# Expert blocks of 64 rows, four rounds of routing and a list-scheduled tail in a graph-layer kernel

## The chip, the cores and the metric

The kernel runs on one core of a Trainium2 chip. The metric is the device time of one execution in microseconds; the figure for a kernel is the median of several runs. A profile is one further execution with the hardware profiler on. The names of the engines are those of the profile: PE (TensorE, with PEld for its weight loads), DVE (VectorE), ACT (ScalarE), POOL (GpSimd) and SP (SyncE, which only issues DMAs here).

## The reference

One layer on 6,250 nodes of 256 features and 106,250 directed edges that are sorted by their target. It adds a message-passing part and a linear attention to the nodes, and then a feed-forward part in which each node goes to one of 32 experts.

```python
xn = _layernorm(x, axis=-1)
x = x + gnn(xn, edge_index, edge_attr_64, W, b, gamma, beta) + mix(xn[None], Wqkv, Wout, bout)[0]
x = x + ffn(_layernorm(x, axis=-1)[None], router_w, router_b, W1, b1, W2, b2)[0]

# gnn
msgs = jnp.concatenate([node_features[source], edge_features], axis=-1)
msgs = jax.nn.silu(msgs @ W + b)
out = jax.ops.segment_sum(msgs, target, num_segments=N)      # then a layer norm with gamma, beta
# mix: 8 heads of 64; k and v are normalised per head
dots = jnp.einsum('bhnd,bhne->bhde', k, v)
out = jnp.einsum('bhnd,bhde->bhne', q, dots) / n             # then Wout and bout
# ffn: one expert per token
idx = jnp.argmax(xf @ router_w.T + router_b, axis=-1)
h = relu(einsum('nd,ndh->nh', xf, W1[idx]) + b1[idx])        # 256 -> 64
out = relu(einsum('nh,nhd->nd', h, W2[idx]) + b2[idx])       # 64 -> 256
```

## The kernel before

**Tiles and stages.** The nodes lie in 49 tiles of 128 rows; `X` holds the running result and `wide` a second copy of each tile (first the transposed layer norm, later the normalised input of the experts), both in SBUF for the whole time. A first stage makes the layer norm, its transposed form in `wide` and the projection `proj` (stored in DRAM). It also tests whether the edges are laid out as the fast path needs. The result of that test is read into registers, and a branch chooses between `ordered` (the fast path) and `general` (a slow path for any edges).

**The edge loop.** `ordered` walks over 208 groups of 512 edges. Per group SP loads the edge features `ea` (line 1198), POOL gathers four times 128 rows of `proj` (`gat`, line 1213), PE turns `ea` (1229) and multiplies it (`h`, 1356), DVE adds (1360), ACT applies silu (1377). Every second group PE sums messages in two levels (`po`, line 1308, with four column tiles, then `sum`, line 1335). When the last edge of a node tile is through, `close` takes its sum (lines 182 and 617). Since the edges are sorted, tile t closes at about the fraction (t + 1)/49 of the loop.

**Other work between the groups.** After each group `work.step` lets a planner (class `Work`) advance other work, which is written as generators. Each step of a generator yields its estimated cost on PE and on DVE and a delay in groups; a group has a budget of 2.7 us on PE and 3.8 us on DVE (`ALLOWANCE`), which is moved a little between odd and even groups. Budget that is left over is dropped. Indirect DMAs of this work wait in a list `work.pool` and are put on POOL's queue beside the gathers, two after every second gather. The pieces are the attention (25 batches of two node tiles, lines 456 to 504, then `mix`, lines 505 to 541), the chunks of four to six closed tiles (add the attention, line 649 and 650; layer norm; router; rank of each token in its expert, lines 636 to 735), and the rounds.

**Rounds of experts.** The tiles are routed in three rounds, of 24, 16 and 9 tiles. For rounds 0 and 1, `places` gives each expert as many blocks of 128 rows as it needs, the tokens are sent to these rows with an indirect DMA per tile (`send`, line 854), and `experts` computes two blocks at a time: it loads the rows (`xb`, 873) and, per block, an expert's weights by a register value (`wt`, 938) from a table `wtab` that was copied together in DRAM beforehand. `layers` transposes (894, 896), multiplies (`phid` 902, `hid` 911) and multiplies again (`py` 923); the bias is a further matmul (945), and line 953 takes the result, which is stored in `yso` (967). Round 2 is an "own" round: each expert has one block of its own, and its weights stay in SBUF (`own_weights`, loaded on ACT's queue after the edge loop). Its bias is added later, at line 1041.

**The tail.** `collect` fetches the result of each tile with an indirect DMA (1024), adds it to `X` (1049, or 1041 to 1045 in the own round) and stores the tile (1052). All collecting comes after the edge loop. There `work.drain` runs the planner without budgets: in each turn every piece that is due is advanced, in the order of the list, and delays count turns. At the end a count of rows that did not fit is read into registers (`lacking`, 1555), and a second branch (1557) would redo the rounds in `again`.

Of the kernel before, what the change touches and what calls it, by code (L numbers as in the profile page):

```python
# [17 lines left out]
P = 128  # L18
# [13 lines left out]
CHUNKS = (6, 6, 6, 6, 6, 5, 5, 5, 4)  # L32
CH = max(CHUNKS)
FIRST = (3, 6, 10, 10, 10, 10)
AB = 2
BB = 2
LEAD = 3
AHEAD = 4
BESIDE = 2
ALLOWANCE = (2.7, 3.8)  # L40


ROUNDS = ((24, 44), (16, 38), (9, None))
# [11 lines left out]
def kernel(  # L55
# [167 lines left out]
    counting = const.tile([P, 3, P], BF16, name="counting")  # L223
    nc.vector.tensor_copy(counting[:, 2, :], ident)
# [18 lines left out]
    row_of = const.tile([P, NQ], F32, name="row_of")  # L243
    flag = const.tile([1, 1], I32, name="flag")
# [31 lines left out]
    with tc.tile_pool(name="prep", bufs=2) as prep, tc.tile_pool(name="pre_ps", bufs=2, space=PSUM) as pre_ps:  # L276
# [88 lines left out]
        nc.vector.tensor_copy(flag, pb)  # L365
# [43 lines left out]
    WROW = DC * HID + D  # L409
    wtab = dram.tile([NE, P, WROW], F32, name="wtab")  # L410

    def tabulate(engine, e0, e1):
        q = slice(e0, e1)
        a = DC * HID
        engine.dma_start(
            wtab[q, :, :a].rearrange("e p w -> (e p) w"), w1[q, :, :].rearrange("e (p c) h -> (e p) (c h)", c=DC)
        )
        for i in range(BB):
            engine.dma_start(wtab[q, i * HID : (i + 1) * HID, a:], w2[q, :, :])

# [3 lines left out]
    def weights(pool, bank, w):  # L424
# [3 lines left out]
        w.update(kv_w=kv_w, dots=dots)  # L428
        nf = 2 * F // P
        raw = pool.tile([P, nf, D], F32, tag="kv", name="raw", bufs=2)  # L430
        nc.sync.dma_start(raw, wqkv[F:, :].rearrange("(f p) c -> p f c", p=P))
        rawr = pool.tile([NE, D], F32, tag="sq", name="rawr")
# [3 lines left out]
        for f in range(0, nf, 2):  # L436
            pt = bank("t", [P, DC, 2, P], "pt")
            for c in range(DC):
                for i in range(2):
                    nc.tensor.transpose(pt[:, c, i, :], raw[:, f + i, c * P : (c + 1) * P], ident)  # L440
            nc.scalar.copy(kv_w[:, :, f * P : (f + 2) * P], pt.rearrange("p c i e -> p c (i e)"))
            yield 0.5, 0.0, 0
# [15 lines left out]
    def attention_batch(pool, bank, w, t0, t1):  # L458
# [3 lines left out]
        kv = pool.tile([P, AB, 2, F], F32, name="kv", bufs=2)  # L462
        var = small.tile([P, AB * 2 * HEADS], F32, name="var")
        for j in range(m):
            for s in range(2):
# [5 lines left out]
                nc.scalar.copy(kv[:, j, s, :], b)  # L471
                yield 1.9, 0.0, 1
            sq = pool.tile([P, 2 * HEADS, DH], F32, name="sq")
            nc.scalar.activation(sq, kv[:, j].rearrange("p s (h d) -> p (s h) d", d=DH), AF.Square)  # L474
# [11 lines left out]
        for j in range(m):  # L486
            k = kv[:, j, 0, :].rearrange("p (h d) -> p h d", d=DH)
            nc.vector.tensor_mul(k, k, both[:, j, :, None].to_broadcast([P, HEADS, DH]))
        yield 0.0, 1.4, 1
        pd = bank("t", [P, HP, DH], "pdot")  # L490
        for h in range(HP):
            for j in range(m):
                for i in range(2):
# [3 lines left out]
                        kv[:, j, 0, q],  # L497
                        kv[:, j, 1, q],
# [4 lines left out]
        nc.vector.tensor_add(dots, pd, dots)  # L503
        yield 0.6 * m, 0.4, 0

    def attention_matrix(pool, bank, w):

        raw = pool.tile([P, 2, HP, D], F32, tag="kv", name="raw", bufs=2)
        wq, rawo = raw[:, 0], raw[:, 1].rearrange("p h c -> p (h c)")
# [4 lines left out]
        made = pool.tile([P, 2, HP, D], F32, tag="kv", name="made", bufs=2)  # L514
        qd, wo_t = made[:, 0], made[:, 1]
        diag = pool.tile([P, HP, P], F32, tag="sq", name="diag")
# [26 lines left out]
    class Nodes:  # L543


        def __init__(self, pool, bank, rounds, in_order):
# [10 lines left out]
            self.so_far = pool.tile([P, BB, NE], F32, name="so_far")  # L557
# [4 lines left out]
            most = (N + (P - 1) * NE) // P + BB  # L562
            self.number = pool.tile([BB * NE, most], F32, name="number")
# [7 lines left out]

            self.upto = pool.tile([BB * NE, BB * NE], F32, name="upto")
            self.b2_sb = pool.tile([BB * NE, D], F32, name="b2_sb")
            nc.vector.memset(self.upto, 0.0)
            for i in range(BB):
                q = slice(i * NE, (i + 1) * NE)
                nc.vector.tensor_add(self.upto[q, q], after[q, q], ident[q, q])
                nc.sync.dma_start(self.b2_sb[q, :], b2)
# [24 lines left out]
            self.at = {}  # L603

        def clear(self, r, b0, b1):
            nc.sync.dma_start(
                r.xs[b0 * P : b1 * P, :].rearrange("(b p) d -> p b d", p=P),
                zero[:, None, :].to_broadcast([P, b1 - b0, D]),
# [24 lines left out]

        def chunk(self, t0, t1):
# [11 lines left out]
            for t in range(t0, t1):  # L646
                p = self.bank("kv", [P, D], "pres")
                for c in range(DC):
                    nc.tensor.matmul(p, xnT(t, c), mix[:, c, :], start=(c == 0), stop=(c == DC - 1))
                nc.vector.tensor_add(X[:, t, :], p, X[:, t, :])  # L650
                moments(mv2, t - t0, X[:, t, :])
                yield 0.9, 1.0, 0
            self.at[t0] = 1
            yield 0.0, 0.0, 1
# [3 lines left out]
            yield 0.0, 2.2, 1  # L658
# [64 lines left out]
            nc.tensor.matmul(pr[:, 1, 0, :], ones[0:1, :], self.so_far[0:1, 0, :], start=True, stop=True)  # L723
# [9 lines left out]
            nc.vector.tensor_copy(self.so_far, ahead[:, None, :, m].to_broadcast([P, BB, NE]))  # L733
            nc.vector.tensor_mul(logit, logit, hot)
            nc.vector.tensor_reduce(self.rank[:, t0:t1], logit, axis=AX.X, op=ALU.add)
            yield 1.2, 2.2, 1
            self.at[t0] = 3
            if r.own:
                row = small.tile([P, CH], F32, name="place")
                nc.vector.scalar_tensor_tensor(  # L740
                    row[:, :m], top[:, :m], float(-P), self.rank[:, t0:t1], op0=ALU.mult, op1=ALU.add
                )
                nc.vector.tensor_scalar_add(row[:, :m], row[:, :m], float(NE * P))
# [863 lines left out]
```

## Time and profile before

| | us |
|---|---|
| Median of three runs | 1425.22 |
| Lowest and highest | 1421.08, 1427.03 |
| The profiled execution | 1422.18 |
| Its span, first to last instruction | 1420.5 |
| PE busy | 1118.7 (79%) |
| POOL busy | 939.6 (66%) |
| DVE busy | 851.6 (60%) |
| ACT busy | 541.2 (38%) |
| First gather of the edge loop starts | 103.97 |
| Last gather starts | 1217.50 |
| Last matmul of the attention matrix starts (line 537) | 669.5 |
| Tokens are sent | 40 tiles before the last gather, 5 from 1235, 4 from 1302 |
| Results are fetched (line 1024) | from 1246.23 |
| Last store is issued (line 1052) | 1402.55 |

A row of a group of instructions has the line, engine and operation, what is written from what, how often, the busy time in us and the mean of one in ns, then the time for which the engine was idle just before them and what ended that idleness ("issue": nothing that the profile shows). A row of the order of time has the start, the duration, the instruction and in brackets the idle time before it. A row of the table of stages has a stretch of time, its length, the busy time and the number of instructions of PE, PEld, DVE, ACT and POOL (or of the one engine asked for), the TensorE clock granted (1.00 is full), the busy share of the DMA engines, and GB/s.

### The profile page before, as it was taken

The page shows a single profiled execution, that of the slowest core. Times are in us where ns is not written, and L with a number is a line of the kernel's source. Part 1 is how long each engine was busy: PE and PEld are TensorE (multiplying, and loading weights), DVE is VectorE, ACT ScalarE, POOL GpSimd, SP SyncE. Part 2 cuts the span into 40 slices and gives each one's busy share as a digit, 9 for nine tenths or more (in the row PEclk, how much of TensorE's full clock was granted, in tenths as well). Part 3 has the DMA queues.
Part 4 walks back from the last instruction along what each step waited for, and adds up shares of the span by engine and source line. Part 5 has one row for each costly group of instructions (what it writes and reads, how often), then busy time and mean ns, then how long its engine had stood idle before and what let it go on. Part 6 is the DMA issues. An engine that isn't in the chain of part 4 may idle for free.

```text
span 1420.5 us, 22703 instructions
## 1 busy us (share of the span) xinstructions
PE 1118.7 (79%) x7340; PEld 656.5 (46%) x7340; DVE 851.6 (60%) x2256; ACT 541.2 (38%) x987; POOL 939.6 (66%) x1050
## 2 busy tenths in 40 slices
PE   4876898899988888988987875489889766857862
PEld 3653444445444444545654543255555433534440
DVE  6933766767766676677876773256556644435342
ACT  2543555455445444543333332134344322212120
POOL 3537777777777777777777777777777677316222
PEclk9997999999999999999999877599999797866585
DMA  7238777655555554445444444478887546589672
GB/s 242 78 107 234 203 198 213 198 172 168 160 156 169 159 170 131 130 131 164 133 127 134 132 119 121 143 203 243 250 241 217 139 118 191 160 244 282 210 242 71
DMA packets 251813, 245.16 MB, mean 173 GB/s; under 512 B 130176, under 2 KB 221736, under 8 KB 251676
## 3 DMA queue, kind: packets, MB, share of 16 engines
q0 software_dynamic: 44960, 121.67, 29.3%
q1 hardware_dynamic: 196152, 113.91, 27.3%
q10 hardware_dynamic: 10564, 7.95, 1.9%
q8 instruction: 63, 1.03, 0.3%
q14 instruction: 74, 0.61, 0.2%
HBM read 194.34 MB, written 55.38 MB: 176 GB/s over the span
## 4 chain that ended last, share of the span: by engine, by line


## 5 line engine op out<-in xcount | busy, mean ns | idle before, releaser
L1213 POOL DMA_INDIRECT gat<-proj,src_T x831 | 796.8, 959 | 266.4 <-issue 219.8
L1360 DVE TENSOR_TENSOR gat<-h,gat 128x1024 f32<-128x1024 f32 x208 | 254.1, 1222 | 280.2 <-PE h L1356 148.0
L1377 ACT ACTIVATE gat<-gat 128x1024 f32<-128x1024 f32 x208 | 219.8, 1057 | 242.9 <-DVE gat L1360 205.8
L1356 PE MATMUL h<-ge,eT 64*128 64x256 f32 x1664 | 251.6, 423 | 33.2 <-DVE gat L1360 32.3
L1356 PEld LDWEIGHTS h<-ge,eT 64*128 64x128 f32 x1664 | 155.0, 198 | 137.1 <-issue 98.8
L1335 PE MATMUL sum<-part,s 128*128 128x256 f32 x400 | 129.6, 452 | 93.3 <-DVE s L1324 93.0
L468 PE MATMUL kv<-kv_w,wide 128*128 128x512 f32 x392 | 188.0, 606 | 3.2 <-DVE kv_w L450 3.2
L1233 ACT COPY eT<-pt 128x256 f32<-128x256 f32 x208 | 77.3, 371 | 204.6 <-PE pt L1229 195.0
L1335 PEld LDWEIGHTS sum<-part,s 128*128 128x128 f32 x400 | 78.7, 215 | 144.8 <-DVE s L1324 129.0
L1308 PE MATMUL po<-gat,s 128*32 128x256 f32 x1664 | 130.8, 439 | 0.0
L1024 POOL DMA_INDIRECT ot<-yso,back x49 | 48.5, 990 | 101.3 <-DVE wide L688 28.0
L1317 ACT COPY part<-po 128x256 f32<-128x256 f32 x104 | 38.7, 372 | 187.2 <-PE po L1308 187.2
L1229 PE MATMUL pt<-ident,ea 128*128 128x128 f32 x416 | 93.7, 308 | 2.2 <-DMA ea<-in_edge_attr_dram 1.4
L468 PEld LDWEIGHTS kv<-kv_w,wide 128*128 128x128 f32 x392 | 68.4, 193 | 57.5 <-issue 52.3
L475 DVE TENSOR_REDUCE var<-sq 128x16 f32<-128x1024 f32 x49 | 59.7, 1218 | 52.1 <-ACT sq L474 52.0
L896 DVE COPY xbT<-pt 128x512 f32<-128x512 f32 x57 | 39.2, 688 | 73.9 <-PE pt L894 73.7
L1308 PEld LDWEIGHTS po<-gat,s 128*32 128x32 f32 x1664 | 47.8, 121 | 67.7 <-issue 35.8
L1229 PEld LDWEIGHTS pt<-ident,ea 128*128 128x128 f32 x416 | 42.8, 144 | 75.2 <-issue 50.0
L854 POOL DMA_INDIRECT xso<-wide,slot x49 | 49.3, 1006 | 27.1 <-DVE back L770 16.7
L299 POOL TENSOR_TENSOR X<-X,bo 128x256 f32<-128x256 f32 x49 | 35.5, 746 | 47.7 <-ACT xn L296 25.9
L894 PE MATMUL pt<-ident,xb 128*128 128x128 f32 x228 | 49.2, 349 | 21.6 <-DMA xb<-xso 19.9
L306 PE MATMUL pp<-gw,wide 128*128 128x256 f32 (+1 forms) x196 | 53.5, 417 | 13.8 <-ACT wide L303 6.6
(264 smaller groups left out, 1391.7 us busy)
## 6 DMA issues: line engine op xcount, KB each, us to landing
ea<-in_edge_attr_dram SPq DMA_DIRECT2D x207, 128.0 KB
xb<-xso SPq DMA_DIRECT2D x57, 256.0 KB
xso<-zero SPq DMA_DIRECT2D x28, 512.0 KB
wt<-wtab SPq DMA_DIRECT2D x72, 192.0 KB
gat<-proj,src_T POOLq DMA_INDIRECT x831
yso<-xb SPq DMA_DIRECT2D x41, 256.0 KB
wtab<-in_L_ffn_W_dram SPq DMA_DIRECT2D x24, 256.0 KB
out_dram<-ot SPq DMA_DIRECT2D x48, 128.0 KB
```

What stands on the lines that cost most here:

```text
L306: nc.tensor.matmul(pp[:n, :], xnT(t, c, n), gw[:, c, :], start=(c == 0), stop=(c == DC - 1))
L468: nc.tensor.matmul(b, xnT(t0 + j, c), kv_w[:, c, s * F : (s + 1) * F], start=(c == 0), stop=(c == DC - 1))
L475: nc.vector.tensor_reduce(var[:, j * 2 * HEADS : (j + 1) * 2 * HEADS], sq, axis=AX.X, op=ALU.add)
L854: ins = nc.gpsimd.indirect_dma_start(out=r.xs[:], out_offset=bass.IndirectOffsetOnAxis(ap=self.slot[:n, t : t + 1], axis=0), in_=wide[:n, ...
L1213: nc.gpsimd.indirect_dma_start(out=gat[:n, k % 2, k // 2, :], out_offset=None, in_=proj[:], in_offset=bass.IndirectOffsetOnAxis(ap=src_T[: ...
L1229: nc.tensor.transpose(pt[:, j, :], ea[:, 2 * j : 2 * j + 2, :].rearrange("p k d -> p (k d)"), ident)
L1233: nc.scalar.copy(eT, pt)
L1308: nc.tensor.matmul(po[k * wide_k : (k + 1) * wide_k, :], s1[:, k, :], msg[:, k % 2, k // 2, :], start=(g == here[0]), stop=(g == here[-1]) ...
L1335: nc.tensor.matmul(sums[t], s2[:, (t - lo) * P : (t - lo + 1) * P], part, start=(q == opens[t]), stop=(q == closes[t]),)
L1356: nc.tensor.matmul(h[:, s, j, :], eTs[g][half, j, :], ge[half, :], start=True, stop=True)
L1360: nc.vector.tensor_add(gats[g], h, gats[g])
L1377: nc.scalar.activation(gats[g], gats[g], AF.Silu)
```

## The change

- Expert blocks have 64 rows (`HB`) in place of 128. `layers` works on a quad of four blocks: two tiles of 128 rows, in each of which the upper and lower half belong to different experts. Its matmuls are written to 64 columns of the array each, and the bias matmuls now stand ahead of `py`, in all rounds.
- There are four rounds, of 28, 11, 5 and 5 tiles, with room for 76 and 44 blocks in the first two. The last two are own rounds, with 64 rows for each expert. The chunks are (6, 6, 5, 5, 6, 6, 5, 5, 3, 2).
- The table `wtab` is gone. `experts` loads `w1` and `w2` of each block with two DMAs from the inputs. The own weights are loaded on SP's queue, during the edge loop, into tiles of `wide` whose tokens have been sent.
- `collect` fetches into 12 tiles of `wide`, adds into `X` and stores two tiles with one DMA.
- PE budget of up to 1.5 us is carried to the next group (`CARRY`); some delays of a group are gone; tokens are put on POOL's list as soon as their chunk has its places; the attention's part of later tiles (`mixing`) is added early.
- `drain` keeps a planned time for PE, DVE and POOL. It advances the first piece, urgent ones first, that is due and whose engine is planned to be free within 1 us.
- The branch ahead of the edge loop is gone: the result of the first test and the count of rows that did not fit are added into one flag, which is read after the tail. If it is set, `general` computes all again from the inputs. The arm `again` for the rounds is gone.
- The attention keeps `kv` in four buffers of one tile each in place of two of two tiles, has two buffers for the squares `sq`, and begins a batch a group after the last where it was three.

```diff
-CHUNKS = (6, 6, 6, 6, 6, 5, 5, 5, 4)
+CHUNKS = (6, 6, 5, 5, 6, 6, 5, 5, 3, 2)
+KV = 4
+HB = 64
+QB = 2 * BB
+AHEAD_US = 1.0
+CARRY = (1.5, 0.0)
-ROUNDS = ((24, 44), (16, 38), (9, None))
+ROUNDS = ((28, 76), (11, 44), (5, None), (5, None))
+BACK = (32, 44)
...
-            sq = pool.tile([P, 2 * HEADS, DH], F32, name="sq")
-            nc.scalar.activation(sq, kv[:, j].rearrange("p s (h d) -> p (s h) d", d=DH), AF.Square)
+            sq = pool.tile([P, 2 * HEADS, DH], F32, name="sq", bufs=2)
+            nc.scalar.activation(sq, kv[j].rearrange("p s (h d) -> p (s h) d", d=DH), AF.Square)
...
+        def mixings(self, t0, t1):
+
+            for t in range(t0, t1):
+                if t not in self.mixed:
+                    self.mixed.add(t)
+                    self.mixing(t)
+                    yield 0.9, 0.4, 1
...
+            ph = self.bank("kv", [P, QB // BB, HB], "phid")
+            for j in pairs:
+                for c in range(DC):
+                    for i in range(BB):
+                        nc.tensor.matmul(
+                            ph[i * HID : (i + 1) * HID, j, :],
+                            w1_of(BB * j + i, c),
+                            xbT[:, j, c, i * HB : (i + 1) * HB],
+                            start=(c == 0),
+                            stop=(c == DC - 1),
+                            tile_position=(0, i * HID),
+                        )
...
+                    nc.tensor.matmul(
+                        py[j][i * HB : (i + 1) * HB, :],
+                        one_of(BB * j + i).to_broadcast([NE, HB]),
+                        self.b2_sb,
+                        start=True,
+                        stop=False,
+                        tile_position=(0, i * HB),
+                    )
...
+                    nc.tensor.matmul(
+                        py[j][i * HB : (i + 1) * HB, :],
+                        hid[half, j, :],
+                        w2_of(BB * j + i, half),
+                        start=False,
+                        stop=True,
+                        tile_position=(i * HID, i * HB),
+                    )
...
-                last = queue.dma_start(w[:, i, :], wtab[bass.ds(e, 1), :, :].rearrange("o p w -> p (o w)"))
+                queue.dma_start(
+                    wa[:, b : b + 1, :], w1[bass.ds(e, 1), :, :].rearrange("o (p c) h -> p o (c h)", c=DC)
+                )
+                last = queue.dma_start(
+                    wb[i * HID : (i + 1) * HID, j : j + 1, :], w2[bass.ds(e, 1), :, :].rearrange("o h d -> h o d")
+                )
...
+        def own_weights(self):
+
+            for q in range(NE // QB):
+                e = slice(QB * q, QB * (q + 1))
+                while not all(self.work.turn >= self.gone.get(t, 1 << 30) + 3 for t in range(QB * q, QB * (q + 1))):
+                    yield 0.0, 0.0, 1
+                nc.sync.dma_start(
+                    wide[:, QB * q : QB * q + 2, :].rearrange("p t (b w) -> p (t b) w", b=2),
+                    w1[e, :, :].rearrange("e (p c) h -> p e (c h)", c=DC),
+                )
+                nc.sync.dma_start(
+                    wide[:, QB * q + 2 : QB * (q + 1), :], w2[e, :, :].rearrange("(j i) h d -> (i h) j d", i=BB)
+                )
+                self.weights_in += 1
+                yield 0.0, 0.0, 2
...
             for t, n, ot in got:
...
+                nc.vector.tensor_add(X[:n, t, :], ot[:n, :], X[:n, t, :])
             yield 0.0, 0.5 * len(got), 1
-            for t, n, ot in got:
-                nc.sync.dma_start(out[t * P : t * P + n, :], ot[:n, :])
+            move_rows(nc.sync, X[:, t0:t1, :], t0, t1, out, True)
...
         def drain(self):
+
             self.draining = True
             while self.pool:
-                self.pool.pop(0)()
+                self.issue(self.pool.pop(0))
+            for piece in self.pieces + self.urgent:
+                piece.due = self.now
             while self.pieces or self.urgent:
-                self.step((1e9, 1e9))
+                for piece in self.urgent + self.pieces:
+                    busy = (self.pool_free if piece.on_pool else max(self.free)) - self.now
+                    if piece.due <= self.now and (piece.urgent or busy <= AHEAD_US):
+                        self.advance(piece)
+                        break
+                else:
+                    self.now += 0.2
...
-    unlike = nc.values_load(flag[0:1, 0:1], min_val=0, max_val=1 << 20)
-    with tc.If(unlike < 1) as path:
...
+    with ExitStack() as arm:
+        with tc.manual_schedule():
+            ordered(arm)
+    wrong = nc.values_load(flag[0:1, 0:1], min_val=0, max_val=1 << 20)
+    with tc.If(wrong > 0):
         general()
```

## The prediction

> **What bounds the kernel now.** The chain of waits is empty for this execution, so I read the costliest groups, then the table of stages, then the order of time at both ends.
>
> ```profile
> L1213 POOL DMA_INDIRECT gat<-proj,src_T x831 | 796.8, 959 | 266.4 <-issue 219.8
> ```
>
> The gathers of the edge loop run on POOL; the gap before most of them waits for nothing. POOL's part of the order of time shows the step and the end of the loop:
>
> ```profile
> 1215.00 0.95 POOL L1213 DMA_INDIRECT gat<-proj,src_T  x1 [0.30 <-PE po L1308]
> 1216.25 0.95 POOL L1213 DMA_INDIRECT gat<-proj,src_T  x1 [0.30 <-issue]
> 1217.50 0.89 POOL L1213 DMA_INDIRECT gat<-proj,src_T  x1 [0.30 <-issue]
> ...
> 1235.17 1.05 POOL L854 DMA_INDIRECT xso<-wide,slot  x1 [16.70 <-DVE back L770]
> ```
>
> A gather takes a step of 1.25 us. From 103.97 to 1218.4 POOL does 831 gathers (1039 us) and 40 sends at 1.31 (52 us): 1091 of 1114 us. So POOL paces the loop, 5.0 us a group of four; only 23 us is lost. The stages (us, busy PE, PEld, DVE, ACT, POOL, then clock, DMA share, GB/s):
>
> ```profile
> 920.00:1120.00 200.00, 174.17 (x1289) 105.92 (x1282) 113.60 (x265) 81.84 (x169) 148.01 (x157) 0.95 0.77 225
> ...
> 1246.00:1302.00 56.00, 36.33 (x204) 22.85 (x203) 26.93 (x92) 9.26 (x27) 17.85 (x18) 0.68 0.89 270
> 1302.00:1332.00 30.00, 22.46 (x101) 12.31 (x100) 6.31 (x13) 6.34 (x18) 11.01 (x15) 0.50 0.74 228
> 1332.00:1383.00 51.00, 39.44 (x257) 24.48 (x256) 22.98 (x48) 11.83 (x32) 15.38 (x16) 0.77 0.75 238
> 1383.00:1403.00 20.00, 8.37 (x14) 3.46 (x14) 7.69 (x19) 0.00 (x0) 9.14 (x9) 0.57 0.41 124
> 1403.00:1420.00 17.00, 0.00 (x0) 0.00 (x0) 0.00 (x0) 0.00 (x0) 0.00 (x0) 0.50 0.09 18
> ```
>
> While round 0's experts run (920 to 1120) POOL keeps its step and PE has 26 us left. After 1218 no engine is full, and 202 us pass: round 1's pairs until 1331, the own pairs to 1383, their nine fetches to 1403, then 17 us with no work. This tail is what the change can shorten.
>
> **The skill.** "TensorEngine Tiling (Array Packing)", Tiling Modes (Key Properties), says that tiles of the array run loads and matmuls in parallel and that a change of mode drains TensorE. The trace agrees with the first: from 300 to 400 us, 176 passes of po (four column tiles) keep PE busy 11.78 us, 67 ns each, where 44 passes of sum on the whole array take 12.02 us, 273 ns. No row shows the drain. "TensorE: Matmul & The Clock Gate", Part 1, says that idling PE falls to half its clock: 0.50 stands at 1302 to 1332, and the slowest phid pass is 477 ns against 273. "Runtime: NRT & Kernel Launch", Instruction fetch mechanics, says that a taken branch out of the fetched pages must fetch its target. At the end (line 1557) it shows:
>
> ```profile
> L1557 PEldq COMPARE_BRANCH  x2: 3382/4670/5957, 1403.3 to 1406.9; - x2
> ```
>
> **The change, part by part.** Where the planner places work I count its groups, at 5.0 us each plus 1.31 for each send.
>
> *The first branch goes.* Worth 0. POOL passed it at 96.2 and then waited 11.1 us until 102.41 for DVE's row_of before its first iota, which stays ahead of the first gather. Bounds: 0 to 2 us gained, since the load of ea must land too.
>
> *Attention.* Two sq buffers take away at most the 52.0 us that DVE waited for sq at line 475, and the batches follow each other sooner. DVE and ACT are not the pace there, PE nearly is (494.79 of 566 us). Last mix matmul: 670. Round 0 now closes its tile 27 at about group 119, 104 + 119 x 5 + 15 = 714. Cost 0, hidden by POOL's step; if PE fills up, each us is lost in the loop. Bounds: -5 to +25.
>
> *Tables and clears.* 24 copies of 256 KB go, and the cleared rows fall from 14,592 to 11,776. DMA share is 0.60 there, so 0.
>
> *Expert blocks.* 57 pairs become 46 quads (19 + 11 + 8 + 8). A pair of round 0 costs PE, from the 920 to 1120 rows of its lines: transposes 15.57/21, phid 15.09/22, py 18.57/22, bias 15.92/22, together 3.0 us. A quad has the same transposes (0.74); phid has twice the passes at half the columns (16 x 36 ns, the pace of pdot's 160 passes in 5.76 us: 0.6); bias and py have twice the passes in two tiles each, 0.72 and 0.84 if they overlap, twice that if not. So 2.9 to 4.5 us; I take 3.1, since po shows overlap. SP pays more: a fetched block is two DMAs of 0.355 and a register load, about 0.4 (two fetches took 1.5), so 4 x 1.1 + 0.85 for tokens and result = 5.3 us a quad, against 2.4 a pair. At 8.3 us a pair (22 pairs from 918 to 1100) SP still has room: 5.3 + 0.7 for ea.
>
> *Rounds moved into the loop.* Sends inside it go from 40 to 47 (28 + 11 + 5 + 3): +9 us. Round 1's last tile (38) closes at group 166: 104 + 830 + 37 (28 sends) + 15 = 986; about 60 us to rank and send; 11 quads at 8.3 end near 1140. Round 2's tile 43 closes at group 187, near 1105; ranked by 1140, its 8 quads (weights already in wide) end near 1210. PE over 885 to 1229: 66 groups x 2.9 (h, pt, po, sum) + 38 x 3.1 + 25 for the chunks = 334 of 344 us. It just fits, so I add 2 us of stall. New end of the gathers: 1218 + 9 + 2 = 1229.
>
> *Own weights, mixings, returns.* The own weights move from ACT's queue after the loop (8 DMAs) to SP's inside it (16 DMAs, 16 x 0.36 = 6 us of issue, 4.2 MB over some 200 us), into tiles of wide. Each waits for the sends of its four tiles, and the next loads of ea stand behind it; the planner keeps three groups, 15 us, between, while a send takes 1.31 and lands within a few us: 0, up to 15 if a send is late. The pres matmuls of tiles 28 to 48 (51.4/49 = 1.05 us each, 22 us) run once mix is there, in PE's share of 670 to 860 (158.03 of 190), out of the last chunk's chain; carried PE budget fills such groups too. Returns get 12 buffers for 6, free once DVE has added them, so POOL no longer waits for a store to land (5.6 us in all); 49 stores become 25 or 26, which saves SP 23 x 0.37 = 9 us that other engines cover. All this is in the sums below.
>
> *The tail.* Its chain is now only round 3: (a) last gather to last sum: before 28 us (L617 ends at 1246.7), with experts between; the last group's h came 7 us after the gather, and the closing steps now follow at once, 7 more: 14. (b) Last sum to sends: 56 us before. Its DVE steps are some 35 of 0.16 to 0.6 us, 12 us, plus transposes and hops, 5, plus collect work between, 3: 20. (c) Two sends, landing and token load: 2.6 + 5.4 = 8; round 0 needed 3.2 from token issue to transposes. (d) Eight quads: a pair took 51/16 = 3.2 us at clock 0.77; per quad 3.1 to 5, I take 4: 33 with fill. (e) Last result to last store: 20.1 before for nine fetches (1382.4 to 1402.55), less four at 1.25: 15. (f) What follows: 18 before, one PE branch of 3.4 to 6.0 less: 13. Sum 103, so the span is 1229 + 103 = 1332. The 44 other fetches need 44 x 1.25 = 55 us of POOL, 1229 to 1284, and must let (b)'s sends in: +6 for one that does not. 1338; the profiled run was 1422.18 for a span of 1420.5: 1340. The median stands 3 us above it: **1343**.
>
> What is late next: POOL's fetches end near 1315 with the sends between, so they come 10 us before (e). The own weights no longer load at 1247 to 1263, when the DMA share is 0.89.
>
> **Rivals.** *As above*, 1343, chance 0.50. *A fuller tail*: PE, 97% booked by my sum, does not finish 11 + 8 quads in the loop. If all 19 spill, 19 x 4 = 76 us follow the gathers, where 42 us (a to c) is free: +34, and 6 more for the cold clock: 1383. For: before, round 1's sends came only at 1145, 130 us after its last tile could close. Against: its 16 tiles shared groups with 22 pairs, now 11 share with 19. Chance 0.25. *A shorter tail*: ranking 15, quads at 3.1, branches 6 less, no POOL collision: 1343 - 5 - 7 - 6 - 6 and 10 for better packing: 1309. Chance 0.11. *Slower*: SP's queue. Loads of ea stand in order behind 8 weight DMAs, 4 register loads and waits on ACT (SP waited 143 us for xb at line 967). If a quad holds up the edge loop, 38 of them pay; below 83/38 = 2.2 us each the tail's gain wins, above it the kernel is slower. SP waiting out ACT for 3 us a quad gives 38 x 3 = 114: 1457. For: 5.3 us of issue beside a group of 5.0. Against: ea is loaded four groups ahead, 20 us. Chance 0.14. *Not doing what it says*: a block overflow would run the general path. The router's counts with these inputs are 70 blocks of 76 and 38 of 44, and at most 51 and 45 tokens of 64 for an expert, so no.
>
> **The numbers.** What this measurement can tell from no change is about 0.5%, 7 us. The likeliest has its own range of 1315 to 1372. For 8 in 10 I go to 1303 to 1405: below lies half of the short-tail case, above the slow one. Faster 0.83 (the first three, less 0.03 near the bound), same 0.03, slower 0.14.
>
> **What would show it.** Last gather at 1220 to 1240, 44 to 47 sends before it; L896 done for rounds 0 to 2 by then; last sum 14 us after the last gather; 8 quads in about 33 us; under 14 us after the last store. Wrong if POOL's gathers step over 1.3 us on average while experts run, or if SP's waits stand before ea in PE's idle time.

## The result, and the profile after

The changed kernel takes 1443.38 us (median of four runs, 1439.15 to 1445.90), the kernel before 1426.12 in runs beside it: a ratio of 1.0118, 95% interval 1.0074 to 1.0162. It is slower by 1.2%; the forecast was 1343. The profiled execution took 1439.15 us for a span of 1437.2.

The tail did become shorter, from 202 us after the last gather to 132. But the edge loop ends 87 us later. First POOL's part of the order of time of the changed kernel (start, duration, instruction, in brackets the idle time before it):

```profile
1304.64 0.89 POOL L1223 DMA_INDIRECT gat<-proj,src_T  x1 [0.31 <-issue]
...
1344.77 1.01 POOL L874 DMA_INDIRECT xso<-wide,slot  x1 [6.65 <-DVE back L790]
...
1360.50 1.00 POOL L874 DMA_INDIRECT xso<-wide,slot  x1 [0.23 <-DVE X L1057]
...
1361.80 1.77 POOL L874 DMA_INDIRECT xso<-wide,slot  x1 [0.21 <-issue]
```

The last gather starts at 1304.64 (1217.50 before); the last two tiles are sent 56 us later. The costliest group, with the idle time that POOL has before its gathers:

```profile
L1223 POOL DMA_INDIRECT gat<-proj,src_T x831 | 797.7, 960 | 345.3 <-issue 305.5 <-PE pt L1239 13.4 <-PE h L1363 4.3
```

A gather takes as long as before (960 ns, 959 before). The idle time before gathers rose from 266.4 to 345.3 us, by 79: POOL is no longer the pace of the loop. The table of stages (us, then busy time and instructions of PE, PEld, DVE, ACT and POOL, then clock, DMA share, GB/s) says where:

```profile
200.00:300.00 100.00, 86.29 (x594) 45.63 (x590) 66.98 (x163) 46.90 (x73) 71.45 (x75) 0.91 0.50 139
...
960.00:1160.00 200.00, 151.18 (x1226) 90.59 (x1226) 88.06 (x214) 65.23 (x144) 115.16 (x123) 0.86 0.71 203
...
1373.00:1412.00 39.00, 34.61 (x288) 20.20 (x288) 9.88 (x21) 9.55 (x32) 7.60 (x8) 0.74 0.58 190
1412.00:1428.00 16.00, 0.00 (x0) 0.00 (x0) 1.92 (x5) 0.31 (x1) 5.35 (x5) 0.57 0.31 93
1428.00:1437.00 9.00, 0.00 (x0) 0.00 (x0) 0.20 (x1) 0.00 (x0) 0.00 (x0) 0.50 0.06 17
```

From 960 to 1160, while the fetched experts run, POOL issues 119 gathers and 2 sends (each send has a short `MEMSET` ahead of it, which makes the 123). At steps of 1.25 and 1.31 us that is 151 of 200 us; most of the rest is 12 gaps, 52 us in all. PE is busy for 151 of 200, so no engine is full. In the attention (200 to 300) POOL issues 75 gathers where it issued 80 in the kernel before:

```profile
200.00:300.00 100.00, 87.28 (x620) 46.01 (x612) 66.14 (x154) 47.83 (x76) 75.93 (x80) 0.94 0.69 195
```

By 850 us the changed kernel is 17 gathers behind the kernel before, by 1200 us, sends counted, 49. The last three rows of the changed kernel's table are the end of the tail: round 3's eight quads, then their fetches, then 9 us with next to no work (17 us with none before).

How a group loses its time is seen at 1041 to 1051 us. SP's queue of the changed kernel, from one load of tokens (`xb`) to the next:

```profile
1041.22 0.53 SPq L1208 DMA_DIRECT2D ea<-in_edge_attr_dram  x1
1041.84 0.46 SPq L962 DMA_DIRECT2D yso<-xb  x1
1042.35 0.46 SPq L888 DMA_DIRECT2D xb<-xso  x1
1044.04 0.36 SPq L979 DMA_DIRECT2D w1t<-in_L_ffn_W_dram  x1
1044.64 0.48 SPq L982 DMA_DIRECT2D w2t<-in_L_ffn_W_dram  x1
1045.89 0.36 SPq L979 DMA_DIRECT2D w1t<-in_L_ffn_W_dram  x1
...
1050.58 0.53 SPq L1208 DMA_DIRECT2D ea<-in_edge_attr_dram  x1
1051.16 0.50 SPq L888 DMA_DIRECT2D xb<-xso  x1
```

And PE and POOL of the same stretch:

```profile
1042.89 0.69 PE L918 MATMUL phid<-xbT,w1t 128*64 128x64 f32 x6 [1.80 <-DMA w1t<-in_L_ffn_W_dram]
1046.19 1.13 PE L910 MATMUL pt<-ident,xb 128*128 128x128 f32 x4 [2.61 <-DMA xb<-xso]
1047.11 1.91 PE L1343 MATMUL sum<-part,s 128*128 128x256 f32 x4
1048.95 1.07 PE L1316 MATMUL po<-gat,s 128*32 128x256 f32 x16
```

```profile
1040.86 0.95 POOL L1223 DMA_INDIRECT gat<-proj,src_T  x1 [0.30 <-issue]
1050.45 0.94 POOL L1223 DMA_INDIRECT gat<-proj,src_T  x1 [8.64 <-issue]
```

SP needs 8.8 us from one quad's tokens to the next quad's, 1.8 us of it per block of weights, and there is only one load of edge features (`ea`) between. PE had the transposes of the tokens issued at 1042.35 at the head of its queue and could start them only at 1046.19, having stood for 2.61 us, and for 1.80 us before that for weights. Only then came `sum` (1.91 us, at half pace; the fence of experiment 7 has it at 1.03) and `po` of the edges. `po` is the last reader of the gathered rows, which have six buffers; it ends at 1050.02, and the next gather starts at 1050.45, after 8.64 us of idleness. The profile names no releaser for it, but by the order of the program the gather needs the buffer that `po` has read. So the gather is late through PE's order, and PE through tokens, weights and the amount of work that was put ahead of `po`.

### The profile page after: what moved, and what is told of

Its sections match the earlier page's. It is cut to its first block, busy times and chain, and to the rows that moved or that the text cites. A ratio compares the mean times of both kernels' runs of the same rounds, so it can differ in the third digit from the quotient of the medians.

```text
span 1437.2 us, 24149 instructions
## 1 busy us (share of the span) xinstructions
PE 1131.5 (79%) x7897; PEld 665.6 (46%) x7897; DVE 837.9 (58%) x2264; ACT 545.1 (38%) x1013; POOL 939.7 (65%) x1050
## 3 DMA queue, kind: packets, MB, share of 16 engines
q8 instruction: 66, 1.08, 0.3%
## 5 line engine op out<-in xcount | busy, mean ns | idle before, releaser
L1223 POOL DMA_INDIRECT gat<-proj,src_T x831 | 797.7, 960 | 345.3 <-issue 305.5
L1363 PE MATMUL h<-ge,eT 64*128 64x256 f32 x1664 | 258.3, 432 | 32.2 <-DVE gat L1365 31.6
L1363 PEld LDWEIGHTS h<-ge,eT 64*128 64x128 f32 x1664 | 159.4, 204 | 138.3 <-issue 97.3
L912 DVE COPY xbT<-pt 128x512 f32<-128x512 f32 x46 | 31.6, 688 | 104.8 <-PE pt L910 100.1
L476 DVE TENSOR_REDUCE var<-sq 128x16 f32<-128x1024 f32 x49 | 59.4, 1217 | 50.2 <-ACT sq L475 50.2
L1036 POOL DMA_INDIRECT wide<-yso,back x49 | 48.2, 984 | 55.2 <-DMA yso<-xb 33.6
L910 PE MATMUL pt<-ident,xb 128*128 128x128 f32 x184 | 39.5, 348 | 49.2 <-DMA xb<-xso 46.8
L472 ACT COPY kv<-kv 128x512 f32<-128x512 f32 x98 | 56.1, 573 | 18.8 <-PE kv L469 18.1
```

The source lines that it names most:

```text
L472: nc.scalar.copy(kv[j][:, s, :], b)
L476: nc.vector.tensor_reduce(var[:, j * 2 * HEADS : (j + 1) * 2 * HEADS], sq, axis=AX.X, op=ALU.add)
L910: nc.tensor.transpose(pt[:, j, c, :], feats[:, c, :], ident)
L1223: nc.gpsimd.indirect_dma_start(out=gat[:n, k % 2, k // 2, :], out_offset=None, in_=proj[:], in_offset=bass.IndirectOffsetOnAxis(ap=src_T[: ...
L1363: nc.tensor.matmul(h[:, s, j, :], eTs[g][half, j, :], ge[half, :], start=True, stop=True)
```

## The experiments

All are edits of the changed kernel, unless the text says otherwise. The first four were made to tell three causes apart: TensorE is full, SP's queue, and the pace at which the planner hands out work.

**1. No weights fetched after the fourth quad.**

```diff
-            wa = pool.tile([P, QB, DC * HID], F32, name="w1t", bufs=4)
-            wb = pool.tile([P, QB // BB, D], F32, name="w2t", bufs=4)
-            for b in range(QB):
...
+            if len(kept) < 4:
...
+                kept.append((wa, wb))
+                blocks = range(QB)
+            else:
+                wa, wb = kept[b0 // QB % 4]
+                blocks = range(0)
+            for b in blocks:
```

> Left out: from the fifth quad of rounds 0 and 1 on, the two weight DMAs and the register load of each block; these quads multiply with the weights of an earlier quad. TensorE does the same instructions. Theory 1 (SP's issue of the fetches, about 1.8 us a block and 8.7 us a quad in the profile, holds back the loads of xb and ea behind it, and TensorE waits in order): the last gather comes back from 1305 us to 1235 to 1255 us, TensorE's wait for xb falls from 47 us to under 15, and the time to 1375 to 1395. Theory 2 (TensorE is full: a quad costs 3.6 us and not the 3.1 of the prediction, and 38 of them plus the edge work do not fit): the last gather stays after 1285 us and the time above 1420.

Measured: 1403.91 us in one run beside 1425.38 for the kernel before; last gather at 1267.7, 37 us earlier than in the changed kernel. PE's waits for `xb` fall from 47 to 22 us. The work on PE is the same, so a full TensorE isn't the cause. The fetches are a part of it, and not the whole: the loop still ends 50 us later than before. The edit takes away both their issue on SP and the waits for them to land, and does not divide the two.

**2. Every second block's weights on ACT's queue.**

```diff
-                queue = nc.scalar if i and self.in_order and self.work.draining else nc.sync
+                queue = nc.scalar if i and self.in_order else nc.sync
```

> The weights of every second block are fetched on ACT's queue in the edge loop too, not only after it. Theory 1 (SP's issue is the pace of the quads): SP's time for a quad falls from 8.7 to about 5 us, the last gather comes 30 to 60 us earlier than 1305 and the time falls to 1385 to 1415. Theory 2 (TensorE is full): within 8 us of 1443. A third one (ACT now waits for free weight buffers in order and holds up silu): slower than 1443.

Measured: 1457.38 us (ratio to the kernel before 1.0221, interval 1.0188 to 1.0255), last gather at 1323.1. PE waits only 7.1 us for `xb`, and yet the loop is 18 us longer. ACT, which the edges need in every group, is now held up: it stands 37.2 us before its copies to `eT` until DMAs of `w2t`, and from 850 to 1220 us PE waits 49 us for ACT (5 us in the changed kernel). To relieve SP at the expense of an engine on the path is no gain.

**3. Three groups between a quad's loads and its transposes.**

```diff
-            yield 0.0, 0.0, 1, 3.5
+            yield 0.0, 0.0, 3, 3.5
...
-            yield 0.0, 0.0, 1, 3.0
+            yield 0.0, 0.0, 3, 3.0
```

> The planner lets three groups pass, not one, between the loads of a quad and its transposes, in all rounds; nothing else is changed. If what costs is only that TensorE meets transposes whose rows have not landed (latency, not SP's throughput), TensorE's wait for xb (47 us) goes and the last gather comes back by 30 to 50 us, to 1255 to 1275, with a time of 1395 to 1415. If SP's throughput is the pace, four quads in flight only fill its queue: less than 20 us gained. If TensorE is full, nothing is gained.

Measured: 1415.10 us (0.9921, 0.9874 to 0.9968), last gather at 1266.1, PE's wait for `xb` 12 us. A later start of the transposes regains 38 us of the loop.

**4. The old pace: no carried budget, batches of the attention three groups apart.**

```diff
-CARRY = (1.5, 0.0)
+CARRY = (0.0, 0.0)
...
                     batches.append(work.add(attention_batch(attn, bank, w, t, min(t + AB, NT))))
-                    yield 0.0, 0.0, 1
+                    yield 0.0, 0.0, 3
```

> Only the planner's pacing of the first half is put back: no PE budget is carried from group to group, and an attention batch begins three groups after the last. In the changed kernel 8 gathers are missing at 300 us and 19 at 850 us against the kernel before. If the carried budget and the batches in step with each other are the cause, the lag at 850 us falls to under 8 gathers and the time by 10 to 25 us, to 1420 to 1433. If the cause is something else (the earlier mixing, the buffers of kv), the lag stays and the time is within 6 us of 1443, or later by what the rounds start later.

Measured: 1394.08 us (0.9779, 0.9745 to 0.9814), last gather at 1226.7. This is 49 us faster than the changed kernel and faster than the kernel before. The edit was thought of for what is lost by 850 us (17 gathers, 21 us), but it regains 78 us of the loop, most of them in the experts' stage. So the pace is the largest of the three. Which of its two edits?

**5 and 6. Each alone:** in 5 only the line of `CARRY` is changed, in 6 only the delay of the batches.

> The changed kernel with one of the two pacing edits undone: PE budget that a group leaves over is dropped again (CARRY 0), the attention's batches still begin a group apart. Theory 'carried budget': with 1.5 us carried, a group may be handed up to 4.2 us of other PE work, more than one group of 5 us can take beside its own 2.9, so PE falls behind in the attention and in the experts' stage alike; then this kernel gets nearly all that the two edits gave together: 1395 to 1405 us, last gather near 1230, 850 us reached with 593 to 596 gathers (581 in the changed kernel). Theory 'batches in phase': the loss begins with the batches that start a group apart and come in bursts; then this gains little, 1430 to 1440, and 850 us still shows 580 to 585 gathers.

> The changed kernel with the other of the two pacing edits undone: the attention's batches begin three groups apart again, PE budget is still carried. Theory 'carried budget': the attention gains some of its 24 us, the experts' stage none, so 1420 to 1440 us, last gather at 1280 to 1300. Theory 'batches in phase': most of the gain of the two together (49 us) comes from here, 1395 to 1410, last gather near 1230 to 1245.

Measured: 5 takes 1393.18 us (0.9806, 0.9748 to 0.9864), last gather at 1221.5; 6 takes 1436.21 (1.0094, 1.0058 to 1.0131), last gather at 1300.4. The carry alone is worth 50 us; the pace of the batches is worth nothing that can be told from the changed kernel's own interval. At 850 us, 5 is 13 gathers ahead of the changed kernel. (50 us is the difference of the medians; the two ratios to the kernel before, 0.9806 and 1.0118, give 44.) The stages of 5:

```profile
200.00:300.00 100.00, 87.49 (x625) 46.94 (x626) 66.33 (x157) 48.58 (x76) 75.94 (x80) 0.93 0.52 146
...
960.00:1160.00 200.00, 170.89 (x1394) 99.86 (x1396) 103.43 (x249) 75.87 (x162) 145.66 (x163) 0.87 0.78 227
```

POOL is back at 80 in the attention, as before. Its 163 instructions in the experts' stage are 141 gathers, 11 sends and their 11 `MEMSET`s: at 1.25 and 1.31 us 191 of 200 us, with 11 us in gaps where the changed kernel has 52. PE does more in these 200 us, 1394 passes in place of 1226. SP's queue of the same kernel, again from one quad's tokens to the next quad's:

```profile
1015.16 1.08 SPq L1208 DMA_DIRECT2D ea<-in_edge_attr_dram  x2
1016.33 0.46 SPq L962 DMA_DIRECT2D yso<-xb  x1
1016.84 0.46 SPq L888 DMA_DIRECT2D xb<-xso  x1
...
1025.26 1.07 SPq L1208 DMA_DIRECT2D ea<-in_edge_attr_dram  x2
1026.43 0.48 SPq L962 DMA_DIRECT2D yso<-xb  x1
1026.96 0.46 SPq L888 DMA_DIRECT2D xb<-xso  x1
```

A quad still takes SP 10.1 us here, but now two groups of edges go by (`x2` loads of `ea`) where one went by in the stretch with the carry. Over the whole stage the difference is smaller, but of the same sign, as is seen when the passes of phid (16 to a quad; a pair before has 8) and the gathers from 960 to 1160 us are counted:

| | quads or pairs | gathers | quads per group of 4 gathers |
|---|---|---|---|
| Before (pairs) | 18 | 145 | 0.50 |
| Before with the carry, experiment 7 (pairs) | 18 | 139 | 0.52 |
| Changed | 17 | 119 | 0.57 |
| 1, no fetch | 19 | 128 | 0.59 |
| 2, ACT's queue | 17 | 113 | 0.60 |
| 3, three groups | 16 | 126 | 0.51 |
| 4, no carry, batches apart | 16 | 139 | 0.46 |
| 5, no carry | 17 | 141 | 0.48 |
| 6, batches apart | 18 | 115 | 0.63 |
| 8, no carry, batches apart, three groups | 16 | 143 | 0.45 |

The quads get done at nearly one rate, 16 to 19 in 200 us, in all these schedules; what sets it was not tested, and without the fetches it is 19. What the carry changes is how few edges go by meanwhile. It puts more quads into a group, but no more into a microsecond.

**7. The kernel before, with the carry.**

```diff
-            self.left = [min(left, 0.0) + more for left, more in zip(self.left, allowance)]
+            self.left = [min(left, kept) + more for left, kept, more in zip(self.left, (1.5, 0.0), allowance)]
```

> The kernel before with one edit of the change alone: PE budget of up to 1.5 us is carried to the next group. Its experts are pairs of 128-row blocks, its fetches one DMA per block, its attention batches three groups apart. Theory 'carried budget': the carry does harm by itself, whatever the size of the blocks: 1440 to 1465 us, last gather at 1235 to 1260 (1217.5 before). Theory 'carry with quads': the carry does harm only where the experts' steps are longer than their planned cost and SP is slow to load, so here it is within 5 us of the kernel before.

Measured: 1441.43 us (1.0136, 1.0083 to 1.0189), last gather at 1241.4. So the carry costs 17 us by itself, with pairs of 128-row blocks and one DMA per block: the first theory holds, near its lower end. Here is a group of it on PE, and the gather after it:

```profile
985.55 0.98 PE L669 MATMUL lg<-rw_t,xfT 128*128 128x32 f32 x8
986.36 0.63 PE L681 MATMUL pt<-ident,wide 128*128 128x128 f32 x4
986.92 1.09 PE L923 MATMUL py<-wt,hid 64*128 64x256 f32 x4
987.95 0.70 PE L945 MATMUL py<-b_sb,choseno 32*128 32x256 f32 x4
989.12 0.66 PE L902 MATMUL phid<-xbT,wt 128*64 128x128 f32 x8 [0.47 <-ACT xb L953]
989.71 0.75 PE L894 MATMUL pt<-ident,xb 128*128 128x128 f32 x4
990.29 1.03 PE L1335 MATMUL sum<-part,s 128*128 128x256 f32 x4
991.25 1.07 PE L1308 MATMUL po<-gat,s 128*32 128x256 f32 x16
```

```profile
992.74 0.94 POOL L1213 DMA_INDIRECT gat<-proj,src_T  x1 [4.12 <-issue]
```

No wait of note stands in this group. The router and steps of several pairs, 4.7 us of other work, simply stand ahead of `sum` and `po`; from one `h` (984.21) to the next (992.25) PE needs 8.0 us in place of 5.0, and POOL idles for 4.12 us where 0.30 is usual. From 960 to 1160 us POOL's gaps add up to 30 us, where the kernel before has 12. A group with `sum` is given 1.6 us of PE budget and one without 3.8. The carry may add 1.5 us to either, beside the 2.9 us that the edges need on the mean, in a step of 5.0 us; and the planner begins a step as long as both budgets are above zero, so a group can go over them.

**8. No carry, batches and transposes three groups apart** (the edits of 3 and 4 together).

> Both pacing edits undone (CARRY 0, batches three groups apart) and tokens waited for three groups instead of one before a quad's transposes are put on PE's queue. If the waits for tokens (17.7 + 6.0 us on PE with the old pacing) still hold up the loop, this gains 5 to 15 us on the 1394 of the old pacing: 1380 to 1390. If the old pacing has already removed what the longer delay removed (28 us on the changed kernel), it is the same within 4 us, and if later quads spill into the tail it is 5 to 10 us slower.

Measured: 1391.33 us (0.9789, 0.9728 to 0.9850), last gather at 1226.7. Between 4, 5 and 8 there is no difference that these intervals can show. What the longer delay gave with the carry (28 us) is not there without it.

**9 to 12, and their repeats.** Four more kernels were to divide the cost of the carry: carried only until the attention's matrix is made (9), no carry and no fetch (10), the carry kept and quads handed out two groups apart (11), half the carry (12).

In 9, `step` reads `self.carry`, which starts as `CARRY`, and `attention` ends with

```diff
                 attn_scope.close()
+                work.carry = (0.0, 0.0)
```

10 has the edits of experiments 1 and 5. In 11 `round` is changed:

```diff
                 last = self.work.add(quad)
-                yield 0.0, 0.0, 1
+                yield 0.0, 0.0, 2
```

And in 12:

```diff
-CARRY = (1.5, 0.0)
+CARRY = (0.75, 0.0)
```

> The changed kernel, in which PE budget is carried only until the attention's matrix is made (about 690 us); from then on what is left over is dropped, as in the kernel before. It divides the 50 us that the carry costs. If the cost is one of each stage, the attention keeps its loss (about 8 gathers by 300 us, 10 to 15 us of time) and the rest is regained: 1403 to 1412 us, last gather near 1235 to 1245. If the experts' stage suffers only because the attention came late, this stays above 1430.

> No carried budget, and from the fifth quad of the fetched rounds on no weights are loaded and no registers are read (the quads use the weights of earlier ones). It prices SP's issue once the budget is not carried. Theory 'SP's queue sets the pace of the quads, the carry sets how many are asked for': with one quad per two groups SP's 9 to 10 us a quad fit beside the edges, so little is left to gain before the last gather (within 10 us of 1221), and what is gained comes from quads that no longer spill: 1370 to 1390. Theory 'SP is a cost of its own': another 30 us and more go, as between the changed kernel and the one without the fetch (35 us): 1350 to 1365.

> The changed kernel with the carry kept; a round hands out its next quad two groups after the last, in place of one. In the trace of the changed kernel SP issues one load of edge features per quad at 1020 to 1060 us, without the carry two per quad. Theory 'too many quads per group for SP': this brings two loads per quad back whatever PE's budget, so the experts' stage regains most of its 60 us, the attention keeps its loss: 1400 to 1415 us, last gather near 1235 to 1255. Theory 'the carry overbooks PE with all kinds of work': 1425 to 1443, last gather at 1280 or later.

> The changed kernel with half the carry, 0.75 us. If every carried us costs, in proportion, this lies half way: 1410 to 1425 us, last gather near 1260. If only what exceeds PE's and SP's room costs, half the carry is nearly free, and because it packs the loop better it may be the fastest: 1380 to 1400.

In these runs and in all their repeats the kernel before took 1827 to 1863 us in place of 1425. The expected times, which are for the pace of the first eight, can't be compared with what came:

| | median, us | ratio to the kernel before in runs beside it, with interval |
|---|---|---|
| 9, repeat | 1914.75, 1905.70 | 1.0273 (1.0209 to 1.0337), 1.0283 (1.0140 to 1.0425) |
| 10, repeat | 1845.21, 1840.20 | 0.9882 (0.9821 to 0.9943), 0.9955 (0.9919 to 0.9991) |
| 11, three repeats | 1917.54, 1914.10, 1905.48, 1899.08 | 1.0293 (1.0235 to 1.0352), 1.0319 (1.0187 to 1.0451), 1.0420 (1.0353 to 1.0487), 1.0448 (1.0369 to 1.0528) |
| 12, repeat | 1900.91, 1888.96 | 1.0206 (1.0142 to 1.0271), 1.0166 (0.9996 to 1.0336) |

For the last repeat of 11 it was written:

> The changed kernel with the carry kept; a round hands out its next quad two groups after the last, in place of one. From 960 to 1160 us the changed kernel and the one without the carry both do 17 quads (272 passes of phid), but the former only 119 gathers beside them and the latter 141. Theory 'too many quads per group for SP': the experts' stage regains most of its 60 us whatever PE's budget, the attention keeps its loss: 1400 to 1415 us, last gather near 1235 to 1255, and again 16 to 18 quads in these 200 us with 130 gathers or more beside them. Theory 'the carry overbooks PE with all kinds of work': 1425 to 1443, last gather at 1280 or later, below 125 gathers.

The kernel without the carry and the changed kernel were not run at that pace, so not even the order within the table says what each edit regains. Four questions stay open: how the 50 us divide between attention and experts when only one of them carries, whether quads further apart would do as well as no carry, whether half the carry is harmless, and what SP's fetch costs without the carry. For the last, the trace of 5 argues that nothing is left to gain before the last gather, since POOL's steps fill 191 of 200 us from 960 to 1160; that is argued, and not shown by a run.

## Why the prediction was wrong

The span is 99 us longer than the 1338 of the prediction: some 76 of it is the edge loop (its last gather ends at 1305.5, forecast 1229) and 23 the tail.

**The step that failed** is in "Own weights, mixings, returns": "carried PE budget fills such groups too ... All this is in the sums below". I counted the carry as a help to the packing and gave it no price. Its measured price is 50 us (experiment 5 against the changed kernel; 83 us of the loop, of which a tail that is 32 us longer gives back a part), and 17 us in the kernel before. The condition was written down under Attention, "if PE fills up, each us is lost in the loop", but only for the batches, and bounded at +25. It holds for every group. POOL's step is the pace, a gather is bound to `po` of a group shortly before, and POOL has no spare time to catch up in: what a group needs beyond 5.0 us is lost once the buffers are used up, and the next one, with less on PE, gives nothing back. The gaps of POOL from 960 to 1160 us show it: 52 us in the changed kernel, 11 without the carry. A budget that was left over in one group is no room in the next. My sum of PE over the whole stretch (334 of 344 us) could not see this, because it adds groups that are too full to groups that are not.

**A second step was mis-sized**: "5.3 us a quad" of SP and "11 quads at 8.3". SP takes 8.8 to 10.1 us a quad, not 5.3: I took 0.4 for a register load from the two fetches of a pair, while a block takes 1.8 us from one `w1t` to the next (0.36 and 0.48 for the two DMAs, 0.27 and 0.16 for the register's load and arithmetic; the rest is small steps and time between them). Quads come at 200/17 = 11.8 us, not 8.3. So in the kernel without the carry, where the loop ends at 1221.5 and POOL keeps its step (I had 1229, with more sends), only 23 quads are through by then (368 passes of phid), and 23 of 46 stand in the tail, not 8. Its 1393 us lie near the rival of the fuller tail, 1383, in which 19 quads of rounds 1 and 2 spill; 15 did.

Point by point:

- *The first branch, worth 0*: right; nothing was gained. The first iota of the tokens starts at 104.07 us (102.41 before) and still waits for DVE's `row_of`, 11.02 us.
- *Attention, cost 0*: right for what was meant. Batches a group apart and the second buffer for the squares cost nothing without the carry (1393 in experiment 5, 1394 in experiment 4). DVE still waits 50.2 us for the squares at line 476 (52.0 before), so the two buffers didn't take away what I gave as their most.
- *A quad on PE, 3.1 us*: it takes 0.74 (transposes), 0.69 (phid), 1.08 (bias) and 1.08 (py), 3.6 us at full clock, in the range of 2.9 to 4.5. Overlap was assumed as with `po`, from "TensorEngine Tiling (Array Packing)", Tiling Modes (Key Properties) in the Trainium skill. The gain is less than that: eight passes of bias or py take 1.08 us, 135 ns each, where the kernel before has four of the same length in 0.70, 175 ns each. In both kernels two passes start within 10 ns of each other (1301.01 and 1301.02 in the changed kernel); in the kernel before the two blocks of a pair lie in different rows of the array and already ran side by side. So a pass gains only a factor of 1.3, and twice the passes cost more than before.
- *Sends in the loop, 47*: 44 in the changed kernel, whose loop is longer, and 39 in the kernel without the carry.
- *The tail, 103 and 6*: 132.6 from the start of the last gather. (a) last gather to last sum 10.8 (I had 14); (b) last sum to the last sends 45.1 (20), the one that failed. Round 2's eight quads, which I had placed in the loop, run from 1309 to 1368, beside the ranking, on the engines that it needs, with the fetches of the earlier rounds on POOL; that this is why it takes so long was not tested. (c) 13.0 (8), at whose end PE waits 4.36 us for `xb`; (d) eight quads in 38.4 (33), with waits for `xb` of about 1 us twice, and two quads whose passes of bias and py took 1.97 us for 1.08; (e) 16.6 (15); (f) 8.7 (13).
- *One PE branch left*, from "Runtime: NRT & Kernel Launch", Instruction fetch mechanics: it takes 3.75 us and starts at 1411.4, while PE's last matmul runs. POOL's fetches start 4.6 us later and end after it, so it costs nothing, and (f) is shorter than I had it. That the time goes into fetching the target is not shown by the trace.
- *The clock of an idle PE*: the row that I cited for it, 1302 to 1332 at 0.50, has PE busy for 22.46 of 30 us, so it doesn't show idleness. The row without a pass, 1403 to 1420, has 0.50 too.

**The rivals.** The slower case, SP's queue with 3 us a quad held up, gave 1457, the nearest to the result. Its place and its decision point (2.2 us) were well put, and experiment 1 shows its part, 37 us of the loop. But it lacked what pulls the trigger: beside two groups SP's 10 us a quad fit, beside one they don't, and the carry moves the mix (0.57 quads a group in place of 0.48). And what I held against it, "ea is loaded four groups ahead", was beside the point: in its transposes of `ea` PE waited 0.7 us for `ea` in all; the edges lost their time behind a quad's transposes, which waited 46.8 us for `xb`. How much of the 50 us is SP's queue and how much PE's budget stays open: a later start of the transposes (experiment 3) regains 38 us of the loop with the carry in place, and experiment 11, which was to decide, can't be compared.

**What can be had.** The change without the carry takes 1393 us: 2% less than the kernel before and 3 to 3.5% less than with it (1393.18/1443.38 = 0.965, by the ratios to the kernel before 0.969). The shorter tail of the change is real; it was given back in the loop.

## What to carry to other kernels

Where one engine with a fixed step paces a loop and the others feed it through a few buffers, the time of a group is a maximum, not a sum that evens out: a planner's budget for other work has to hold in each group, and what a group leaves over is gone. Sum an in-order queue (SP's too) per group at the rate at which work will be handed out, register loads and the time between instructions included, and read the rate off the trace: if a stage does the same number of quads in 200 us with any schedule, handing them out faster only makes the groups longer. And price every line of a change, also the one that looks like a mere help to the schedule; it was one constant that cost 50 us.

## What the runs showed of the hardware

- A DMA whose address comes from a register costs SP far more than its own 0.36 or 0.48 us: with the register's load a block of two takes 1.8 us.
- Passes of 256 columns on 32 or 64 rows, which start two at a time in both kernels, take 135 ns each with 64 columns of the array (eight in 1.08 us) and 175 ns each with 128 (four in 0.70 us).
- The same kernel can take very different times: the kernel before took 1424 to 1426 us beside the first eight experiments and 1827 to 1863 beside the others, with a clock of about 0.80 in place of 0.88, and a gather was as long as ever (946 ns in the median in the traces of both). It isn't shown to be the chip: the slower runs were on chips numbered 0, 2 and 12 (1859 and 1863, 1835, 1827 us), and experiments 1 to 4, with 1425, were on number 12 too. In the slower ones, DVE, ACT and SP stand still together and go on at the same instant, as in this order of time of the last repeat of experiment 11; what holds them isn't in the trace.

```profile
314.60 0.42 DVE L504 TENSOR_TENSOR dots<-pdot,dots 128x256 f32<-128x256 f32 x1 [7.98 <-remote]
314.72 11.28 SPq L1208 DMA_DIRECT2D ea<-in_edge_attr_dram  x2
314.78 0.37 ACT L1243 COPY eT<-pt 128x256 f32<-128x256 f32 x1 [7.28 <-remote]
```
